# Two places for the softmax's scores, half banks on half chunks, a select in place of a mask product, and products of zeros on TensorE

## The chip, the cores and the metric

The kernel runs on one core of a Trainium2 chip. The core has a matrix engine (TensorE, PE in the profile), a vector engine (VectorE, DVE), an activation engine (ScalarE, ACT), a general engine (GpSimd, POOL), and a queue engine that issues most of the transfers (SyncE, SP). Each engine works through its own list of instructions in order. They meet through semaphores. TensorE reads from SBUF and writes its sums to PSUM, which has eight banks of 512 f32 columns on 128 partitions.

The metric is device time in microseconds. The times shown are medians of several runs. One further execution was profiled, and all views of the profile come from that one.

## The reference

The input is one sequence `x` of 2048 tokens with 128 features. Four blocks follow each other, each fed by a layernorm and added to `x`:

1. A state space mixer with 8 heads, 16 states and a convolution of 4 taps, with a gate.
2. Causal attention with 16 heads of 8 features, then a mixture of 8 experts. The block normalises its input once more, attends, adds, normalises again, and adds for each token the two experts that its router picks. All eight experts are computed and weighted, with zero for those not picked. An expert is 128 to 512 features, an exact GELU, and back to 128.
3. A Mamba scan with 256 channels and 16 states.
4. A gated network with ternary weights: two products 128 to 512 multiplied with each other, two layers 512 to 512 with GELU, and one back to 128.

What matters most here is the attention:

```
scores = where(causal, q @ k.T / sqrt(8), finfo.min)   # 16 heads, 2048 x 2048
out    = softmax(scores) @ v
```

and the fourth block:

```
h = silu(lin(x, w1)) * lin(x, w2)
h = gelu(lin(h, h1)); h = gelu(lin(h, h2)); return lin(h, w3)
```

## The kernel before, in words

The tokens are cut into four chunks of 512 (`C`). The kernel's functions are `ssd(c)` for block 1, `prepare`, `shift`, `weighted` and `conclude` for the attention, `experts(c)`, `scan(c, part)` on halves of 256 tokens, and `feed(c)` for block 4.

**The order is planned.** The functions do not issue instructions. They record operations in a `Program`, which notes which operation needs which. `Order.play` (line 534) then plays a simple timeline: each operation has a price from `_cost` (line 343), each engine takes the ready operation that can start first, and among equals the one with the longest chain behind it. Tiles get their place when their first operation is taken, so places of SBUF and PSUM are part of this play. The outcome is one fixed list per engine, which `Order.issue` (line 630) emits from line 638. That is why almost all instructions in the profile stand on line 638, and why they have to be told apart by their tiles. On the chip the lists do not change: where an instruction waits, everything behind it on its engine waits too.

**Attention.** For each chunk `c` and each group `g` of four heads there are two loops.

- `shift` (line 869) finds the row maxima. A pair of heads gives two products with 32 rows each into the tile `m` (two banks, one place). On diagonal blocks two bf16 products with `mask_qk` are added. VectorE reduces the 1024 columns to `top_a`.
- `weighted` (line 901) computes the scores again with keys on the partitions. A pair of heads takes the two products `ps_e<-qR,w_kR`, two more that add the shift (`ps_e<-sh,w_onesR`), and on diagonal blocks two bf16 products with `mask_kq`. ScalarE's exponential takes the tile `e` (two banks, **one** place) to `probs` (three places). After both pairs of a key block, four products `ps_o<-probs` add up the weighted values in the bank `o`, in `sum_up` (line 908).

An f32 product is recorded as two matmuls. In the profile `32*128` means that 32 rows of the array were used, `128*9` that 9 columns were.

**PSUM.** `m` and `e` have two banks each, `o` one. Three single banks `a`, `b` and `c` serve everything else, one tile per bank. The banks of `m`, `e` and `o` are lent to these when nobody waits for them (lines 665 to 700).

**SBUF.** The pool `second` (experts and scan) opens after `first` (block 1). The pool `last`, which holds all tiles of `feed`, opens after `attention` has been given up, so no `feed` can start before the attention has ended.

**Scan.** For each of 16 states VectorE multiplies and scans (`sdb`), GpSimd copies the last column (`hlast`), and a GpSimd transfer adds the result to one of two sums (`sL<-sdb`, 256 KB each). GpSimd's list also holds two short operations of each layernorm (`rs`).

The masked product and the exponential in `weighted`, which the change touches most:

```
for j in range(2 * diag):
    nc.tensor.matmul(pss[:, j, q0 : q0 + P], ident16, mask_kq, start=False, stop=True)
pr = tile_("probs", (P, 2, C))
nc.scalar.activation(pr[:, :, q0:], pss[:, :, q0:], AF.Exp, scale=...)
```

Of the kernel before, what the change touches and what calls it, by code (L numbers as in the profile page):

```python
# [76 lines left out]
class Place:  # L77


    def __init__(self, pool, banks=None, lent=None, real=None):  # L80
        self.pool, self.lent, self.real = pool, lent, real
        self.user, self.free = None, 0.0
        self.banks = banks or (self,)


class Tile_:


    def __init__(self, tag, shape, dtype, name, real=None):
# [3 lines left out]
        self.ops = set()  # L93
# [104 lines left out]
class Op:  # L198
    __slots__ = (
        "n", "engine", "calls", "deps", "time", "after", "table", "batch", "allots", "tiles",  # L200
        "rank", "waits", "outs", "start", "end", "ready",
# [3 lines left out]
class Program:  # L205
# [5 lines left out]
    def __init__(self, nc):  # L211
        self.nc, self.ops, self.tags, self.joined, self.batching = nc, [], {}, None, None
        for e in self.ENGINES:
            setattr(self, e, Engine(self, e))
# [14 lines left out]
    def add(self, engine, method, args, kw):  # L229
# [12 lines left out]
        for v, w in [(v, False) for v in reads] + [(v, True) for v in writes]:  # L242
# [21 lines left out]
            t.ops.add(op)  # L264
            op.tiles.add(t)
# [6 lines left out]
    def new(self, engine, table=None):  # L272
# [4 lines left out]
        op.n, op.deps, op.allots, op.tiles = len(self.ops), {}, [], set()  # L277
        self.ops.append(op)
        return op
# [104 lines left out]

class Order:
# [8 lines left out]
    def settle(self):  # L394
# [36 lines left out]
        for op in ops:  # L431
            for t in op.allots:
# [22 lines left out]
    def rank(self):  # L455
        ops = self.p.ops
        outs = {o: [] for o in ops}
        for o in ops:
# [3 lines left out]
            o.ready = 0.0  # L462
# [30 lines left out]
        for o in reversed(order):  # L493
# [5 lines left out]
            o.rank = r + o.after  # L499

    def possible(self, op):

        at, seen, taken = 0.0, {}, set()
        for t in op.allots:
# [7 lines left out]
            for pl in tag.places:  # L512
                if pl in taken or any(b.user is not None or b in taken for b in pl.banks):
                    continue
# [19 lines left out]
    def play(self):  # L534
        free = {e: 0.0 for e in Program.ENGINES}
        cand = {e: [] for e in Program.ENGINES}
# [13 lines left out]
        while len(self.order) < n:  # L550
            best = None
            for e, ops in cand.items():
# [3 lines left out]
                for o in ops:  # L556
                    at = max(free[e], o.ready)
# [10 lines left out]
                    if at < least:  # L568
                        least = at
                    pick.append((at, o))  # L570
                if not pick:
                    continue
                o = max((o for at, o in pick if at <= least + 1e-6), key=lambda o: self.key(o, open_batch))
# [8 lines left out]
            at, o = best  # L582
            e = o.engine
            cand[e].remove(o)
            for t in o.allots:
                t.tag.wanted -= 1
            if o.allots:
                self.possible(o)
                for t in o.allots:
                    t.tag.given += 1  # L590
                    for b in t.place.banks:
                        b.user = t
# [11 lines left out]
            o.start = at  # L604
            free[e] = at + time
            o.end = at + time - o.time + o.after
# [12 lines left out]
            for d, full in o.outs:  # L619
                d.waits -= 1  # L620
                d.ready = max(d.ready, o.end if full else o.start)
                if d.waits == 0:
                    enter(d)
            self.order.append(o)
        self.span = max(o.end for o in self.order)

# [14 lines left out]
SWITCH, BOOST = 1.28, 40.0  # L641
# [3 lines left out]
def two_layers(ctx: ExitStack, tc: tile.TileContext, a: dict, out: bass.AP):  # L645
# [19 lines left out]
    def banks(tag, bank, lent=None, width=1, shared=False):  # L665
        t = nc.tag(tag, width * C, True, shared)
        t.places.append(Place(None, bank.banks if isinstance(bank, Place) else tuple(bank), lent, None))
        return t.places[-1]

    pairs_ = {k: ps.tile([P, 2 * C], F32, name=f"ps_{k}") for k in ("m", "e")}  # L670
    single = {k: ps.tile([P, C], F32, name=f"ps_{k}") for k in ("o", "a", "b", "c")}
    bank = {}
    for k, t in pairs_.items():
        for j in range(2):
            bank[f"{k}{j}"] = Place(None, real=t[:, j * C : (j + 1) * C])
    for k, t in single.items():
        bank[k] = Place(None, real=t)

    def seat(tag, names, lent=None, width=1, shared=False, whole=None):
        t = nc.tag(tag, width * C, True, shared)  # L680
        pl = Place(None, tuple(bank[n] for n in names), nc.tags[lent] if lent else None)
        pl.real = whole if whole is not None else bank[names[0]].real
        t.places.append(pl)

    seat("m", ("m0", "m1"), width=2, whole=pairs_["m"])
    seat("e", ("e0", "e1"), width=2, whole=pairs_["e"])
    seat("o", ("o",))
    for n in ("a", "b"):
        seat("a", (n,), shared=True)
# [839 lines left out]
```

## Time and profile before

| | |
|---|---|
| median of 3 runs | 1730.93 us (1716.0 to 1738.16) |
| profiled execution | 1727.12 us, span 1725.4 us |
| mean granted TensorE clock | 0.785 |
| PE busy | 1503.1 us (87%), 6350 matmul records |
| DVE busy | 994.8 us (58%) |
| ACT busy | 642.9 us (37%), 56 table loads among it |
| POOL busy | 326.4 us (19%) |
| transfers | 91.75 MB, 53 GB/s mean |

The span is the time from the first to the last instruction; the profiled execution took 1.7 us more. "Busy" of PE counts the whole duration of each matmul record, including the time until its result has left the array, so 87% busy does not mean that the array streams for 87% of the time. The granted clock tells which share of its full rate TensorE was given.

Going by the tiles in the trace, block 1 alone fills the first 150 us. Attention runs from there to 1395 us, beside the rest of block 1 and beside experts and scans of chunks whose attention is done. The row maxima (`shift`) end at about 1210 us. From 1395 us on the kernel computes the last experts, the last two scan halves, and all four feeds.

### The profile page before, as it was taken

Reading aid. Unit: us, or ns where it says so; the run is one execution under the profiler, and the core shown is the slowest. Engines: PE = TensorE matmul, PEld = TensorE weight load, DVE = VectorE, ACT = ScalarE, POOL = GpSimd, SP = SyncE. Lnnn points to the kernel's source line nnn. Section 1 sums busy time; section 2 is a strip of 40 time slices with the busy share of each in tenths; the row PEclk is TensorE's granted clock in tenths of the full one; section 3 lists DMA queues with packets and bytes.
Section 4 is the critical chain, followed back from the end, with each engine's and each line's share of the span. In section 5 each row is a group of like instructions: output and inputs, shape, how many; then the busy total and the mean of one; then the engine's idle time right before and its main releaser. Section 6 shows DMA issues by size and latency. Waiting matters only on the chain. (4 is left out here: it accounts for less than half of the span.)

```text
span 1725.4 us, 17368 instructions
## 1 busy us (share of the span) xinstructions
PE 1503.1 (87%) x6350; PEld 670.9 (39%) x6350; DVE 994.8 (58%) x1874; ACT 642.9 (37%) x873; POOL 326.4 (19%) x458
## 2 busy tenths in 40 slices
PE   6899998999999998899998899899877679995738
PEld 3554554455423343333333243233322234442323
DVE  4556557665545468667867656775454551256641
ACT  2221421432334426445453433454445433234311
POOL 4321310310000111212311111121031221103320
PEclk9887987996879959987865655799565569997769
DMA  2000000000112102524402311341042543134730
GB/s 86 1 1 1 1 1 1 1 1 1 42 36 61 51 1 56 123 67 87 97 7 46 60 36 35 95 110 42 13 84 56 99 110 98 49 114 106 157 88 6
DMA packets 77334, 91.75 MB, mean 53 GB/s; under 512 B 7040, under 2 KB 47776, under 8 KB 77248
## 3 DMA queue, kind: packets, MB, share of 16 engines
q1 hardware_dynamic: 59536, 58.11, 11.4%
q0 software_dynamic: 17280, 31.46, 10.7%
q10 hardware_dynamic: 432, 1.06, 0.2%
q8 instruction: 50, 0.82, 0.2%
q14 instruction: 36, 0.29, 0.1%
HBM read 57.90 MB, written 1.25 MB: 34 GB/s over the span
## 5 line engine op out<-in xcount | busy, mean ns | idle before, releaser
L638 DVE TENSOR_REDUCE top_a_None<-ps_m 128x2 f32<-128x1024 f32 (+3 forms) x320 | 339.7, 1062 | 285.0 <-PE ps_m L638 278.4
L638 ACT ACTIVATE probs_attention<-ps_e 128x1024 f32<-128x1024 f32 (+3 forms) x320 | 286.5, 895 | 526.9 <-PE ps_o L638 281.2
L638 PE MATMUL ps_e<-qR_attention,w_kR_attention 32*128 32x512 f32 (+3 forms) x640 | 187.8, 581 | 82.5 <-ACT probs_attention L638 80.9
L638 PE MATMUL ps_m<-w_kR_attention,qR_attention 32*128 32x512 f32 (+3 forms) x640 | 178.3, 546 | 17.4 <-DVE top_a_None L638 16.1
L638 PE MATMUL ps_o<-probs_attention,w_vv_attention 128*9 128x512 f32 (+3 forms) x1152 | 182.6, 712 | 0.2 <-ACT probs_attention L638 0.2
L638 POOL DMA_DIRECT2D sL_second<-sdb_second x114 | 99.2, 885 | 385.6 <-DVE sdb_second L638 328.6
L638 PEld LDWEIGHTS ps_e<-qR_attention,w_kR_attention 32*128 32x128 f32 x640 | 74.0, 227 | 237.9 <-ACT probs_attention L638 187.5
L638 DVE TENSOR_TENSOR_SCAN sdb_second<-sda_second,w_hlast_None,sdb_second 128x256 f32<-128x256 f32 x212 | 149.6, 739 | 7.7 <-ACT sda_second L638 5.4
L638 PEld LDWEIGHTS ps_m<-w_kR_attention,qR_attention 32*128 32x128 f32 x640 | 71.6, 217 | 211.8 <-issue 67.9
L638 PE MATMUL ps_e<-sh_attention,w_onesR_attention 32*128 32x512 f32 (+3 forms) x640 | 148.6, 459 | 0.0
L638 PE MATMUL ps_c<-h_second,fc_second 128*128 128x512 f32 x208 | 114.9, 654 | 0.6 <-DVE ye_second L638 0.6
L638 ACT ACTIVATE sda_second<-sL_second 128x512 f32<-128x512 f32 x120 | 72.7, 624 | 31.8 <-DVE sdb_second L638 18.6
L638 ACT ACT_TABLE_LOAD x56 | 71.8, 1283 | 30.2 <-PE ps_a L638 18.6
L638 DVE TENSOR_TENSOR sdb_second<-sL_second,sbb_second 128x512 f32<-128x512 f32 x101 | 68.0, 680 | 24.0 <-DMA sL_second<-sdb_second 11.1
L638 PEld LDWEIGHTS ps_e<-sh_attention,w_onesR_attention 32*128 32x128 f32 x640 | 80.8, 249 | 0.5
L638 POOL TENSOR_TENSOR acc_second<-acc_second,ye_second 128x512 f32<-128x512 f32 x28 | 36.5, 1305 | 231.3 <-DVE ye_second L638 229.8
L638 PE MATMUL ps_a<-enT_second,fc_second 128*128 128x512 f32 x128 | 77.0, 686 | 3.1 <-ACT h_second L638 2.2
L638 ACT ACTIVATE h_second<-ps_a,cols 128x512 f32<-128x512 f32 x64 | 44.0, 687 | 63.3 <-PE ps_a L638 63.2
L638 POOL COPY w_hlast_None<-sdb_second 128x2 f32<-128x2 f32 x99 | 55.6, 570 | 23.8 <-DVE sdb_second L638 23.5
L638 PE MATMUL ps_b<-enT_second,fc_second 128*128 128x512 f32 x98 | 58.8, 686 | 0.9 <-ACT h_second L638 0.8
L638 PE MATMUL ps_m<-fh_last,hw_last 128*128 128x512 f32 x120 | 58.3, 608 | 0.2 <-DVE sW_second L638 0.2
L638 PEld LDWEIGHTS <-ident 128*128 128x128 bf16 x512 | 30.6, 101 | 61.7 <-issue 50.0
(430 smaller groups left out, 2094.3 us busy)
## 6 DMA issues: line engine op xcount, KB each, us to landing
sL_second<-sdb_second POOLq DMA_DIRECT2D x114, 256.0 KB, 3.6
fc_second<-in_fc SPq DMA_DIRECT2D x64, 256.0 KB, 2.6
sbb_second<-scratch_b SPq DMA_DIRECT2D x112, 128.0 KB, 3.0
gb_second<-scratch_g SPq DMA_DIRECT2D x32, 256.0 KB, 3.3
hw_last<-in_h SPq DMA_DIRECT2D x8, 1024.0 KB, 5.3
w_last<-in_w SPq DMA_DIRECT2D x12, 256.0 KB, 3.9
sbb_last<-scratch_b SPq DMA_DIRECT2D x16, 128.0 KB, 3.4
sL_second<-sdb_last POOLq DMA_DIRECT2D x6, 256.0 KB, 4.2
```

What stands on the lines that cost most here:

```text
L638: getattr(engine, method)(*args, **kw)
```

## The change

It has these parts.

- **Two places for `e`.** PSUM now has `m` (2 banks), `e` (4 banks, two places), `o` and `a`. The banks `b` and `c` are gone.
- **Half banks on half chunks.** A new tag `d` is half a bank (256 columns). `experts` and `feed` now work on 256 tokens at a time, `experts(c, part)` and `feed(c, part)`, and load their weights for each half. `feed` takes its weights in tiles of 256 KB (`fw`, three places in each pool) in place of 1 MB, and has places in `second` as well as in `last`.
- **Mask by a select.** The two `mask_kq` products are left out. After the exponential, GpSimd's `affine_select` sets the masked part of `probs` (128 by 2 by 128) to zero. `mask_qk` in `shift` stays.
- **Products of zeros.** The planner gets a model of the array (`Array`): how many of the array's cells each product uses, in windows of 3.41 us, and a clock that falls to half when the use is low. Where its PE would stand idle and the use of the last window is below `FILL` = 0.7, it puts in a bf16 product of the identity with 512 columns of zeros into a free bank. The built list has 467 of them: 375 go to the bank `a`, 75 to banks of `m`, 15 of `e`, 2 of `o`. 276 stand before the last attention product and 191 behind it.
- **Work moves from VectorE to ScalarE.** The last step of each layernorm, the copies and bias additions out of PSUM in `prepare`, `shift`, `weighted`, `conclude`, `scan` and `feed` become activations. Layernorm gets two more short GpSimd operations (`nm`). One scaling in `scan` goes from VectorE to GpSimd.
- `prepare` is split: the projections of the last two head groups (`project(c, 2)`) come when the chunk's attention starts. `qR` has two places in place of three.

All engines' lists are planned anew. Instructions in the built lists, before and after: ScalarE's table loads 56 and 81, the fetches of expert weights (256 KB each) 64 and 128, PE's bf16 products with a mask 512 and 256. The weights of `feed` were 8 fetches of 1 MB and 12 of 256 KB; they are 104 of 128 or 256 KB.

```diff
-    pairs_ = {k: ps.tile([P, 2 * C], F32, name=f"ps_{k}") for k in ("m", "e")}
-    single = {k: ps.tile([P, C], F32, name=f"ps_{k}") for k in ("o", "a", "b", "c")}
+    wide = {k: ps.tile([P, n * C], F32, name=f"ps_{k}") for k, n in (("m", 2), ("e", 4))}
+    single = {k: ps.tile([P, C], F32, name=f"ps_{k}") for k in ("o", "a")}
...
+    for j in (0, 2):
+        seat("e", (f"e{j}", f"e{j + 1}"), whole=wide["e"][:, j * C : (j + 2) * C])
     seat("o", ("o",))
...
+    for n, lent in (("a", None), ("m0", "m"), ("m1", "m"), ("e3", "e"), ("e2", "e"), ("e1", "e"), ("e0", "e"), ("o", "o")):
+        seat("a", (n,), lent)
+        for half in range(2):
+            seat("d", (n,), lent, half)
...
     def layernorm(z, dst, src, width=D):
...
+        nc.gpsimd.tensor_tensor(nm, mv[:, :, 0], rs, ALU.mult)
+        nc.gpsimd.tensor_scalar(nm, nm, -1.0, None, ALU.mult)
         for b in range(nb):
-            nc.vector.tensor_scalar(
-                dst[:, b, :], src[:, b, :], mv[:, b, 0:1], rs[:, b : b + 1], ALU.subtract, ALU.mult
+            nc.scalar.activation(
+                dst[:, b, :], src[:, b, :], AF.Identity, bias=nm[:, b : b + 1], scale=rs[:, b : b + 1]
             )
...
-                        nc.tensor.matmul(pss[:, j, q0:], onesR[hr], sh[hr, q0:], start=False, stop=not diag)
-                    for j in range(2 * diag):
-                        nc.tensor.matmul(pss[:, j, q0 : q0 + P], ident16, mask_kq, start=False, stop=True)
+                        nc.tensor.matmul(pss[:, j, q0:], onesR[hr], sh[hr, q0:], start=False, stop=True)
                 pr = tile_("probs", (P, 2, C))
...
+                if diag:
+                    select(pr[:, :, q0 : q0 + P], [[0, 2], [1, P]], 0, -1, ALU.is_ge, 0.0)
...
+class Array:
+    WINDOW = 3.41333
...
+            use, part = self.use.get(i - 1, 0.0) / self.WINDOW, self.part.get(i - 1, 0.0) / self.WINDOW
+            fast = FAST or use + 0.6 * part >= 0.33 if self.clocks[i - 1] == 1.0 else use >= 0.37
+            self.clocks[i] = 1.0 if fast else 0.5
...
+                if e == "tensor" and FILL and pe_left > 0 and self.zeroed(last_at):
+                    tf = max(pe.end + FGAP, last_at)
+                    if least > tf and pe.lately(tf) < FILL:
+                        for pl in self.p.tags["a"].places:
...
+                                spare = pl
+                                if best is None or tf < best[0]:
+                                    best = (tf, None)
...
     def filler(self, place):
...
+        op.calls = [("matmul", (t.view(), *self.zeros), {"start": True, "stop": True})]
...
-    def feed(c):
+    def feed(c, part):
...
+            if f % 2 == 0:
+                w12 = tile_("fw", (P, 2, 2 * P))
...
     for c in range(NC):
-        experts(c)
+        for part in range(SPLIT):
+            experts(c, part)
         for part in range(SPLIT):
             scan(c, part)
-        feed(c)
+            feed(c, part)
```

## The prediction

> **What bounds the kernel now.** I read the page first. TensorE (PE) is the busiest engine, 87%, and the row of its granted clock is full of fives and sixes.
>
> ```profile
> PE 1503.1 (87%) x6350; PEld 670.9 (39%) x6350; DVE 994.8 (58%) x1874; ACT 642.9 (37%) x873; POOL 326.4 (19%) x458
> ...
> PEclk9887987996879959987865655799565569997769
> ```
>
> Windows of 50 us read between 0.50 and 1.00, so I count all lowered time as half clock: the mean of 0.785 gives 2 x 0.215 x 1725 = 742 us of it. Next I cut the span into stretches by what runs in them. Columns: stretch, length, busy us of PE, its matmuls, clock, share of the DMA engines, GB/s.
>
> ```profile
> 0.00:150.00 150.00, 121.87 (x488) 0.87 0.08 25
> 150.00:650.00 500.00, 478.41 (x2494) 0.84 0.06 17
> 650.00:900.00 250.00, 226.69 (x960) 0.83 0.34 74
> 900.00:1100.00 200.00, 178.46 (x712) 0.55 0.23 47
> 1100.00:1210.00 110.00, 106.95 (x458) 0.93 0.33 81
> 1210.00:1395.00 185.00, 138.49 (x562) 0.55 0.30 60
> 1395.00:1550.00 155.00, 140.44 (x373) 0.94 0.34 96
> 1550.00:1725.40 175.40, 111.82 (x316) 0.79 0.42 93
> ```
>
> By 2 x (1 - clock) x length, half-clock time is 39, 160, 85, 180, 15, 167, 19 and 74 us. 900:1100 and 1210:1395 run at half clock almost throughout, though PE is busy for 89% and 75% of them. They hold thin attention products and hardly any dense expert products. The stretch between them, with dense products among the same attention, has 0.93. What the low clock costs is seen in the groups of these stretches, first 900:1100, then 1100:1210 (busy us, mean ns):
>
> ```profile
> L638 PE MATMUL ps_m<-w_kR_attention,qR_attention 32*128 32x512 f32 x96 | 36.0, 747 | 3.0 <-DVE top_a_None L638 3.0
> L638 PE MATMUL ps_o<-probs_attention,w_vv_attention 128*9 128x512 f32 x152 | 34.0, 982 | 0.0
> L638 PE MATMUL ps_e<-qR_attention,w_kR_attention 32*128 32x512 f32 x86 | 32.0, 742 | 14.4 <-ACT probs_attention L638 14.1
> ```
>
> ```profile
> L638 PE MATMUL ps_m<-w_kR_attention,qR_attention 32*128 32x512 f32 x62 | 16.2, 520 | 0.3 <-DVE top_a_None L638 0.3
> L638 PE MATMUL ps_o<-probs_attention,w_vv_attention 128*9 128x512 f32 x72 | 11.1, 694 | 0.0
> L638 PE MATMUL ps_e<-qR_attention,w_kR_attention 32*128 32x512 f32 x40 | 10.9, 540 | 1.3 <-ACT probs_attention L638 1.2
> ```
>
> Per pair of heads (two records of m or e, four of o) PE is busy 0.75, 0.89 and 0.74 us in the first, 0.52, 0.62 and 0.55 in the second: the same work in 0.71 of the time. Last the waits, in all and in the longest:
>
> ```profile
> POOL sL_second L638 <- DVE sdb_second L638: 328.6, 73, 19.3
> ACT probs_attention L638 <- PE ps_o L638: 281.2, 124, 5.4
> PE ps_e L638 <- ACT probs_attention L638: 81.4, 104, 2.8
> ```
>
> PE's own wait for the single place of e is 81.4 us, 42.4 of it in 1210:1395. So the bound is PE at a low clock until 1395 us. Behind that it is a chain: experts of the last chunk (1399 to 1491), two scan halves (to 1671), feed (to 1722).
>
> **A rule against the change.** PE's longest wait on the exponential is 2.8 us, and in 900:1100 the longest listed is 2.3 us, yet the clock there is 0.55. The Trainium skill, "TensorE: Matmul & The Clock Gate", section "HAM oscillation — how this bites in real kernels", gives the rule that no idle gaps over about 3.4 us keep the clock up. By it zeros in short gaps would bring nothing, and the sum below would come out about 140 us higher. The measured rows decide: here a busy but thinly used array is at half clock.
>
> **The change part by part,** against the profiled span of 1725.4 us (1727.1 with what lies around it; the median shown is 4 us more).
>
> *Clock.* Half-clock time, times PE's busy share there, times the 0.29 that full clock saves: 0:150 39 x 0.8 x 0.29 = 9; 150:650 160 x 0.96 x 0.29 = 45; 650:900 85 x 0.9 x 0.29 = 22; 900:1100 178 x 0.29 = 52, and 8 of its 21 us without PE busy; 1100:1210 4; 1210:1395 138 x 0.29 = 40 and 8 of waits that run at PE's pace. Sum 188. Zeros stand only where the plan expects idle, and only 276 lie ahead of the end of attention, so I take three quarters: **-141**. Ends: 0 (the use stays too low) and -188.
>
> *Zero products.* No row has 512 bf16 columns. Below, the bf16 mask with 128 columns: two in 0.28 us, 0.14 each. Above, an f32 record with 512 columns, which follows the next in 0.43 us at full clock (four records of ps_m in 1.88 us, two in 1.02). I take half the upper, 0.21, since an f32 record streams more than one pass: 467 x 0.21 = 98 us, ends 65 and 200. The cover is 222 us in which PE is not busy. That idle shrinks when the rest gets faster, and 101 of the zeros wait for the reader of their bank (an activation of 0.69 us, say) with PE's whole list behind them, so a quarter comes on the path: **+25**. If the cover is gone, +98.
>
> *Second place of e.* It removes PE's 81.4 us. In 1210:1395 nothing else fills the gap: -34 of 42. Elsewhere -25 of 39, since m and dense products partly follow anyway: **-59**. Late next is the place of probs: three as before, and ScalarE already waits 281 us for ps_o, which frees them. With the sums at 0.62 a pair beside an exponential of 1.02 us that wait is covered at full clock only. Ends: -10 and -81.
>
> *Mask.* 256 products, 41.1 us busy, leave PE: **-30**. 128 selects come to POOL. Selects of 128x128 took 0.29 to 0.48 us; twice the elements lie between 0.29 and 0.97, I take 0.6: 77 us on an engine that is 19% busy. But each stands between exponential and sum, behind whatever POOL waits for: **+10** (0 to the third rival's price).
>
> *Half chunks.* Expert and feed products have 256 columns: two records take the 0.43 us of one (w_u at 256 columns takes 502 and 405 ns for one record against 654 for 512, but those durations include the way out of the array), so no change in streaming. Past 1395 us, half the final feed (46 us, 1674 to 1720) goes ahead, -20; the first scan half needs half the experts (92 us), -25 of at most 46; the clock there, -10: **-55**. Ends: -100, and +100 by the second rival.
>
> *VectorE to ScalarE.* The rows that move add up to 128.6 us. DVE goes to about 890 us with the smaller pieces. ACT gets 129, about 44 for more pieces (128x256 takes 0.47 us, 128x512 0.69: 352 x 0.47 - 176 x 0.69), and 25 table loads of 1.283 = 32: about 850 us. Both fit beside any time above 1300 us. In 650:900 DVE is busy 185 of 250 us, so **-10**; the loads in the last stretch, **+5**. The 80 new short layernorm operations on POOL (0.23 to 0.49 us each, 18 to 39 us in all) are mostly under PE's work.
>
> *Transfers.* SP issues 470 in place of 282. The list puts fetches of `fw` between the scan's `sbb`; one waiting for its place holds those behind it. I cost this at nothing before 1395 us, where the DMA share stays at 0.34.
>
> Sum: -141 + 25 - 59 - 30 + 10 - 55 - 10 + 5 = -255, so 1727 - 255 = **1472**, rounded to 1470 us.
>
> **The rivals.**
>
> *Half clock stays.* The list is fixed. If the chip runs behind the plan, PE is not idle where the zeros stand, and a stretch that falls to half runs there until dense products come, as before from 1300 to 1400 us, where two windows of 50 us read 0.50. For: between the zeros lie runs of hundreds of attention products. Against: experts come in eight portions in place of four, so dense products are spread. With a third of the clock term (47 of 141) and half of the zeros on the path (49 in place of 25): 1472 + 94 + 24 = **1590**.
>
> *Transfers bound the last stretch.* Feed weights come twice, +11.5 MB, and the last experts +4.2 MB. After 1395 us 155 x 96 + 175 x 93 = 31 MB moved; 47 MB in 275 us is 170 GB/s, more than the densest fortieth of the span (157). The chain that ended last shows what a loaded queue does (start, length):
>
> ```profile
> 1633.42 4.98 DMA sL_second<-sdb_second
> ...
> 1644.60 5.19 DMA sL_second<-sdb_second
> ```
>
> The median landing of these sums is 3.6 us. The last two states' products on VectorE started at 1655.57 and 1661.41, 5.8 us apart, where their work is 0.69 + 1.39 = 2.1. If the 28 sums of the last two halves go so, they add 28 x 3.7 = 104 us in place of the 55 gained: 1472 + 55 + 104 = **1630**.
>
> *Slower: selects behind POOL's waits.* POOL waits 328.6 us in 73 waits for the scan's VectorE work, 4.5 us each. In the new list many selects stand right behind such a transfer. While one waits, ps_o waits, and with it all that follows on PE. If each of the 128 selects costs 2.0 us more than in my sum, the gain of 255 is gone; from 2.3 us on the change is slower by over 2%. At 2.9 us: 1472 + 371 = **1840**. Against: a quarter of the selects belong to the first chunk, where no scan runs yet.
>
> *It does not do what it says:* two places, but ScalarE waits for probs instead. Then 49 of the 59 stay: 1520, inside my case.
>
> *Better:* full clock throughout and PE closer packed, 1330: the busy time at full clock, 1503 - 742 x 0.29 - 41 + 98 = 1345, is near that floor.
>
> **How the numbers follow.** Forecast 1470 (1390 to 1540): 0.45. Half clock stays, 1540 to 1650: 0.22. Transfers, 1540 to 1680: 0.10. Better, under 1390: 0.10. Slower: 0.09. Unmoved, by parts that cancel: 0.04. The range from 1350 to 1680 leaves out some 0.06 below and 0.13 above. Within 2%, 1696 to 1766, is about what a measurement here can tell from no change: 0.04. Faster 0.87, slower 0.09.
>
> **What would show it.** Right: a clock of 0.88 or more; no stretch of 100 us at 0.55; PE's wait on probs for e under 30 us; zero products near 0.21 us apart; attention ending near 1200 us. Wrong: fives in the clock row between the first and the last expert products; POOL selects idle for long behind DVE sdb with ps_o waiting on POOL; DMA share above 0.7 at the end with states 5 us apart.

## The result, and the profile after

The changed kernel took 1815.1 us (median of 4 runs, 1790.43 to 1830.07), the kernel before 1724.18 us beside it. The ratio is 1.047, with an interval of 1.033 to 1.061: slower, where I had forecast 1470 us. A ratio, here and below, is taken over the executions within 1.5% of the fastest of their kernel, so it is not quite the quotient of the medians.

The profiled execution took 1813.19 us, its span is 1811.5 us and its mean granted clock 0.857 (before: 0.785). First the page, with the same two rows as before, and the group of the zero products (busy us, mean ns, then the idle time of PE just before them):

```profile
PE 1521.4 (84%) x7343; PEld 821.4 (45%) x7393; DVE 908.8 (50%) x1726; ACT 811.4 (45%) x1342; POOL 446.3 (25%) x731
...
PEclk9699977989869999965798766798998889998887
...
L811 PE MATMUL ps_a<-zeros,ident 128*128 128x512 bf16 x338 | 114.7, 451 | 58.8 <-ACT h_second L811 32.2
```

The clock row has lost most of its fives, and VectorE (DVE) and ScalarE (ACT) have nearly the busy times I had worked out (890 and 850). Yet the sum is longer. The windows, cut where the stages changed (stretch, length, the busy us of PE, of its weight loads, of DVE, ACT and POOL, then clock, share of the DMA engines, GB/s):

```profile
900.00:1100.00 200.00, 172.27 (x852) 80.86 (x859) 120.80 (x197) 106.37 (x161) 45.14 (x79) 0.82 0.30 70
...
1375.00:1600.00 225.00, 170.63 (x664) 119.79 (x670) 91.20 (x191) 86.93 (x174) 62.01 (x95) 0.90 0.51 123
1600.00:1811.50 211.50, 161.62 (x615) 106.19 (x621) 56.11 (x109) 51.27 (x102) 25.32 (x32) 0.84 0.40 99
```

The stretch 900:1100 has 0.82 where it had 0.55. But the last product of the attention ends at 1362 us (before: 1388), not near 1200, and what is left then takes 449 us in place of 338. In those 449 us no engine is busy for more than 76% of the time, and the clock is at 0.87: that stretch waits. Both stretches, from the first weighted sum to the last and from there to the end, in the same columns:

```profile
181.00:1362.00 1181.00, 1030.55 (x5437) 508.44 (x5460) 681.26 (x1196) 616.30 (x961) 292.16 (x491) 0.85 0.24 56
1362.00:1811.50 449.50, 340.05 (x1321) 230.23 (x1331) 155.45 (x325) 144.34 (x288) 94.99 (x143) 0.87 0.47 113
```

The waits, in all, how many, the longest (us). The last answers the 81.4 us of before, the one above it the 281.2 us; the first two are new in this size:

```profile
ACT h_second L811 <- PE ps_a L811: 177.6, 106, 5.3
...
PE ps_a L811 <- ACT h_second L811: 78.9, 102, 1.4
...
ACT probs_attention L811 <- PE ps_o L811: 69.6, 40, 6.2
...
PE ps_e L811 <- ACT probs_attention L811: 38.2, 58, 1.8
```

PE waits 102 times for ScalarE to have read `h`'s bank, and ScalarE 106 times for PE. Two engines that wait for each other at this rate take turns. The timeline shows how, first in an expert's first layer (start, length, engine, instruction, idle time before it and what ended that):

```profile
1262.79 0.84 ACT L811 ACTIVATE h_second<-ps_a,cols 128x256 f32<-128x256 f32 x2 [1.22 <-PE ps_a L811]
...
1263.68 1.13 PE L811 MATMUL ps_a<-enT_second,fc_second 128*128 128x256 f32 x4 [0.87 <-ACT h_second L811]
1264.85 0.84 ACT L811 ACTIVATE h_second<-ps_a,cols 128x256 f32<-128x256 f32 x2 [0.75 <-PE ps_a L811]
...
1265.74 1.13 PE L811 MATMUL ps_a<-enT_second,fc_second 128*128 128x256 f32 x4 [0.93 <-ACT h_second L811]
1266.91 0.84 ACT L811 ACTIVATE h_second<-ps_a,cols 128x256 f32<-128x256 f32 x2 [1.22 <-PE ps_a L811]
```

PE writes both halves of bank `a`, ScalarE reads both, PE writes both again; nothing lies side by side, though with two places PE could fill one while the other is read. In a feed three engines go round in this way, 1.72 us for each turn (from one start of PE to the next, 1687.81 to 1689.53):

```profile
1687.29 0.47 ACT L811 ACTIVATE fs_second<-ps_a,w_half_s_None 128x256 f32<-128x256 f32 x1 [1.79 <-DVE fxn_second L811]
...
1687.81 0.70 PE L811 MATMUL ps_a<-fnT_second,fw_last 128*128 128x256 f32 x2 [1.12 <-ACT fs_second L811]
1688.55 0.42 DVE L811 SCALAR_TENSOR_TENSOR fs_second<-fs_second,ps_a 128x256 f32<-128x256 f32 x1 [1.30 <-PE ps_a L811]
1689.01 0.47 ACT L811 ACTIVATE fs_second<-ps_a,w_half_s_None 128x256 f32<-128x256 f32 x1 [1.25 <-DVE fs_second L811]
1689.53 0.70 PE L811 MATMUL ps_a<-fnT_second,fw_last 128*128 128x256 f32 x2 [1.02 <-ACT fs_second L811]
```

PE's product at 1687.81 writes the half that nobody reads any more (it becomes the `p1` of the next 128 features), and waits for the activation on the other half (the `p1` of these features). VectorE's step at 1688.55 needs only this `p1` and the activation, both done at 1687.76, and waits for PE.

**What the built program says.** A wait on another engine in it names one instruction of that engine. I looked, for each such wait of an instruction that touches PSUM, at what would have to be waited for if only the same addresses counted, then if the whole bank counted, then if the whole PSUM tile counted. Kernel before: 22 waits exist only because a bank is shared (all between ACT and DVE), 33 only because a tile of several banks is. After: **333** for a shared bank, and **190** for a shared tile. An example of the second sort: a score product into columns 0 to 511 of `ps_e`, the first place, waits for the exponential that reads columns 1024 to 2047, the second place. `ps_e` is one tile of four banks.

So both of the new sorts of place have a snag that I had not seen: halves of a bank exclude each other, and so do the two places of the scores. PE's wait on the exponentials fell all the same, from 81.4 to 38.2 us, but nothing came to lie side by side. For the second sort the trace has a plain count: in the changed kernel not one of the 320 exponentials has a score product running beside it, the same as before, when there was one place.

The Trainium skill, "PSUM — Partial Sum Buffer", section "PSUM bank collisions raise a hardware error", asks for waits by bank (and quadrant of partitions), not by address. The 333 waits are of this kind. The 190 between banks of one tile go beyond it. No run here shows what a collision would do.

### The profile page after: what moved, and what is told of

It is laid out like the page before. It is cut to its first block, busy times and chain, and to the rows that moved or that the text cites. A ratio compares the mean times of both kernels' runs of the same rounds, so it can differ in the third digit from the quotient of the medians.

```text
span 1811.5 us, 20345 instructions
## 1 busy us (share of the span) xinstructions
PE 1521.4 (84%) x7343; PEld 821.4 (45%) x7393; DVE 908.8 (50%) x1726; ACT 811.4 (45%) x1342; POOL 446.3 (25%) x731
## 5 line engine op out<-in xcount | busy, mean ns | idle before, releaser
L811 ACT ACTIVATE h_second<-ps_a,cols 128x256 f32<-128x256 f32 x232 | 100.1, 471 | 186.1 <-PE ps_a L811 177.6
L811 PE MATMUL ps_a<-enT_second,fc_second 128*128 128x256 f32 x428 | 142.3, 451 | 34.0 <-ACT h_second L811 29.3
L811 PE MATMUL ps_a<-zeros,ident 128*128 128x512 bf16 x338 | 114.7, 451 | 58.8 <-ACT h_second L811 32.2
L811 PE MATMUL ps_e<-qR_attention,w_kR_attention 32*128 32x512 f32 (+3 forms) x640 | 121.5, 494 | 36.2 <-ACT probs_attention L811 35.4
L811 POOL TENSOR_SCALAR_AFFINE_SELECT probs_attention<-probs_attention 128x256 f32<-128x256 f32 x128 | 60.0, 474 | 312.2 <-ACT probs_attention L811 311.2
L811 POOL TENSOR_TENSOR acc_second<-acc_second,ye_second 128x256 f32<-128x256 f32 x56 | 46.2, 824 | 346.5 <-DVE ye_second L811 330.6
L811 PE MATMUL ps_a<-h_second,fc_second 128*128 128x256 f32 x360 | 115.6, 447 | 13.9 <-ACT h_second L811 7.2
L811 PEld LDWEIGHTS ps_a<-enT_second,fc_second 128*128 128x128 f32 x428 | 80.3, 211 | 82.5 <-ACT h_second L811 50.7
L811 PE MATMUL ps_e<-sh_attention,w_onesR_attention 32*128 32x512 f32 (+3 forms) x640 | 99.8, 399 | 0.0
L811 PEld LDWEIGHTS ps_a<-h_second,fc_second 128*128 128x128 f32 x360 | 72.4, 219 | 41.7 <-ACT h_second L811 12.4
```

What stands on the lines that cost most here:

```text
L811: getattr(engine, method)(*args, **kw)
```

## The experiments

Times are medians. Every kernel was timed beside the kernel before, whose median lay between 1713.7 and 1731.9 us. A difference of two times in the text can carry some of that: by the ratios the 96 us below are 79, the 93 are 99, and the 80 that half chunks cost are 72. The 0.971 of the run with whole chunks is the quotient of the medians; its four executions took 1645.6 to 1691.38 us, so differences from it hold to some 25 us. "Bank" and "tile" count the two sorts of wait in the built program.

| run | us | ratio to before, interval | bank | tile |
|---|---|---|---|---|
| changed kernel | 1815.1 | 1.047 (1.033 to 1.061) | 333 | 190 |
| no zeros, planned anew | 1812.0 | 1.050 (1.037 to 1.062) | 348 | 186 |
| whole chunks | 1681.3 | 0.971, no interval | 81 | 202 |
| banks apart | 1728.3 | 1.006 (1.001 to 1.011) | 127 | 360 |
| one place for the scores | 2104.0 | 1.217 (1.206 to 1.229) | 307 | 264 |
| scores in two tiles | 1719.1 | 1.002 (0.997 to 1.006) | 332 | 59 |
| two tiles, whole | 1609.7 | 0.936 (0.927 to 0.944) | 81 | 66 |
| two tiles, whole, apart | 1529.4 | 0.891 (0.885 to 0.897) | 44 | 142 |
| two tiles, whole, no zeros | 1553.6 | 0.905 (0.897 to 0.913) | 80 | 66 |
| two tiles, apart, half chunks | 1609.5 | 0.933 (0.926 to 0.941) | 125 | 177 |
| all three, no zeros | 1524.5 | 0.886 (0.880 to 0.892) | 49 | 127 |
| all three, mask by products | 1629.3 | 0.947 (0.939 to 0.955) | 47 | 120 |
| all three, one place | 1573.7 | 0.915 (0.907 to 0.922) | 5 | 79 |
| two tiles, same order, apart | 1626.3 | 0.944 (0.939 to 0.949) | 153 | 191 |
| all three, experts halved | 1577.6 | 0.916 (0.910 to 0.922) | 130 | 148 |
| all three, no select, no mask | 1625.3 | 0.944 (0.939 to 0.950) | 43 | 133 |
| all three, VectorE again | 1593.2 | 0.925 (0.919 to 0.930) | 45 | 139 |
| changed, zeros dropped | 1818.3 | 1.046 (1.034 to 1.057) | 345 | 186 |
| all three, zeros dropped | 1540.2 | 0.893 (0.886 to 0.900) | 46 | 139 |

"Two tiles", "whole", "apart" are the edits shown below (scores in two tiles, whole chunks, a free bank first); "all three" has all of them.

**The planner makes a caveat.** Where an edit changes the operations or the rules for places, all lists are planned anew, and the order by itself can move the time by tens of us. Five runs are free of it: each keeps the order of another kernel to the instruction (scores in two tiles, twice; tiles moved in the same order; zeros dropped, twice).

### One part of the change undone

The first four runs undid one part each (the code shows excerpts: `...` marks lines left out in between, and an edit can have further lines around an excerpt). Theory A was that the halves of a bank exclude each other; B that the zeros cost; C the transfers; D the banks taken by the second place.

No zeros:

```diff
-SWITCH, BOOST, BURST, FAST, PAIR, ZMIN, ZWAIT, FILL, FGAP = 1.28, 40.0, 0.0, False, 0.0, 0.0, 0.0, 0.7, 0.03
+SWITCH, BOOST, BURST, FAST, PAIR, ZMIN, ZWAIT, FILL, FGAP = 1.28, 40.0, 0.0, False, 0.0, 0.0, 0.0, 0.0, 0.03
```

> The changed kernel with no product of zeros at all (467 planned ones left out; the rest of the plan is made anew, nothing else is edited). Theory A, two halves of one bank make PE and its readers take turns: the zeros are a side matter; without them PE gets back the 112 us that they streamed, the clock falls from 0.857 towards 0.80 and the real streaming takes some 60 us more again (1142 to about 1200), so the time stays within 40 us of 1815. Rival B, the zeros themselves are what cost: the zeros' 112 us and the 59 us of idle time before them go and the clock matters less: 1700 to 1740.

1811.96 us at a clock of 0.815: within the 40 us of theory A, and not as B.

Whole chunks for experts and feeds:

```diff
-        for part in range(SPLIT):
-            experts(c, part)
+        experts(c)
         for part in range(SPLIT):
             scan(c, part)
-            feed(c, part)
+        feed(c)
```

> The changed kernel with the experts and the feeds on whole chunks again, with the buffers and the weight loads that they had before; the second place of the scores, the select, the zeros and the half banks for the small tiles stay. Theory A (half banks shared): the large tiles fill whole banks, so PE and the readers do not take turns any more; the last stretch falls from 436 us towards the 330 us of before, the whole to 1690 to 1730. Rival C (the weights, fetched twice as often in small pieces, hold the last stretch): the same 1690 to 1730, so this run alone does not tell A from C. Rival B (zeros cost): 1790 to 1830.

1681.27 us, 134 less than the change, a little better than expected. From the end of the attention on 377 us in place of 449.

A free bank first:

```diff
+                now = max(since, *(b.free for b in pl.banks))
+                if tag.psum and tag.shared:
+                    for b in pl.banks:
+                        now = max(now, b.mate.free)
+                    cost = (any(b.mate.user is not None and b.mate not in pl.banks for b in pl.banks), now)
...
+                if best is None or cost < best[0]:
+                    best = (cost, now, pl)
```

> The changed kernel, where a tile that takes one bank or half of one is put into the bank whose other half is unused and that has been free longest, not into the first free place of the list; chunks stay halved, weights are fetched as in the change, zeros stay. In the plan the tiles that stand beside a live tile in the same bank fall from 557 to 303. Theory A: the last stretch falls from 436 us to 340 to 380 us, the whole to 1710 to 1760, and PE's waits on ACT's reads of h, fs and fh fall to half. Rival C (transfers): the last stretch stays at 420 or more, the whole at 1790 to 1830. Rival B (zeros): the same 1790 to 1830.

1728.33 us, 87 less, and the last stretch is 377 us: theory A, with all fetches as in the change, so C is out as its main cause. PE's waits for ScalarE to read `h`, `fs` and `fh` fall from 99.5 to 49.5 us, to half, as theory A had it. (The plan that ran has 280 such tiles, not 303.)

One place for the scores, the other two banks (still in the tile of four) for single tiles:

```diff
-    for j in (0, 2):
-        seat("e", (f"e{j}", f"e{j + 1}"), whole=wide["e"][:, j * C : (j + 2) * C])
+    seat("e", ("e0", "e1"), whole=wide["e"][:, 0 : 2 * C])
...
-    for n, lent in (("a", None), ("m0", "m"), ("m1", "m"), ("e3", "e"), ("e2", "e"), ("e1", "e"), ("e0", "e"), ("o", "o")):
+    for n, lent in (("a", None), ("e2", None), ("e3", None), ("m0", "m"), ("m1", "m"), ("e1", "e"), ("e0", "e"), ("o", "o")):
```

> The changed kernel with one place of two banks for the softmax's scores, as before, and the other two banks given to the single tiles from the start, as before. Theory A (and my forecast's step of 59 us for the second place): attention ends 40 to 80 us later, while the last stretch stays as it is; 1840 to 1890. Rival D (the banks that the second place takes from the other tiles are what the kernel lacks): faster than the change, 1740 to 1790.

2103.95 us: far outside of both. The loss lies in the attention, 1450 us from the first weighted sum to the last in place of 1181; the last stretch is 452 us. 289 us is no price of a second place. What the count of waits offers is that single tiles now lie in the same tile as the scores and exclude them: 264 waits of that sort in place of 190. That is an argument, not a test of this kernel; but it led to the next run.

### The scores in two tiles

```diff
-    wide = {k: ps.tile([P, n * C], F32, name=f"ps_{k}") for k, n in (("m", 2), ("e", 4))}
+    wide = {k: ps.tile([P, n * C], F32, name=f"ps_{k}") for k, n in (("m", 2), ("e", 2), ("f", 2))}
```

> The changed kernel, instruction for instruction in the same order, but the two places of the scores are two tiles of two banks and no longer the two halves of one tile of four banks. Counted in the built program, 190 waits among the engines that touch PSUM name an instruction on another bank of the same tile; here 59 are left. Theory E (the second place is partly undone by such waits: PE's products into one place wait for ScalarE's exp that reads the other): the stretch of the attention, 1181 us, becomes 30 to 80 us shorter, the whole 1735 to 1785. Rival F (ScalarE and PE are in turn there anyway, so that the wait that is left ends at nearly the same moment): within 15 us of 1815.

**1719.05 us, 96 less** (79 by the ratios), with the same instructions in the same order, and better than both theories had it. Of 320 exponentials 98 now have score products beside them. The timeline of this run shows one: the exponential reads the place `f` while PE fills the place `e`. The second view is the changed kernel's: there the exponential reads the second place of `ps_e`, and the product, into the first, starts when the exponential ends.

```profile
609.93 1.02 ACT L811 ACTIVATE probs_attention<-ps_f 128x1024 f32<-128x1024 f32 x1
...
610.33 0.40 PE L811 MATMUL ps_e<-qR_attention,w_kR_attention 32*128 32x512 f32 x2
...
610.56 0.40 PE L811 MATMUL ps_e<-sh_attention,w_onesR_attention 32*128 32x512 f32 x2
```

```profile
640.12 1.04 ACT L811 ACTIVATE probs_attention<-ps_e 128x1024 f32<-128x1024 f32 x1
...
641.22 0.50 PE L811 MATMUL ps_e<-qR_attention,w_kR_attention 32*128 32x512 f32 x2 [1.45 <-ACT probs_attention L811]
```

Its waits on both places of the scores, which add up to 6.0 us for PE (38.2 before the split):

```profile
PE ps_e L811 <- ACT probs_attention L811: 3.5, 8, 0.6
...
PE ps_f L811 <- ACT probs_attention L811: 2.5, 2, 1.6
```

The gain is where theory E had it. From the first weighted sum to the last the attention takes 1101 us in place of 1181; the last stretch is as long as it was, 450 us. Here are both stretches of this run, to be compared with the next kernel's:

```profile
176.00:1277.00 1101.00, 978.45 (x5438) 495.69 (x5462) 679.46 (x1197) 616.12 (x962) 293.98 (x491) 0.89 0.25 60
1277.00:1726.60 449.60, 337.56 (x1317) 228.96 (x1329) 154.85 (x325) 144.59 (x288) 94.52 (x142) 0.88 0.46 113
```

### The same order, tiles moved to other banks

After the plan is made, a pass goes through its order and moves single tiles (the zeros' too) to a free bank where nothing lies beside them. No instruction changes its place in a list.

```diff
+        for t in sorted(tiles, key=lambda t: where[t][0][0]):
...
+                beside = [u for b in pl.banks if b.mate not in pl.banks for x, y, u in used.get(b.mate, ()) if x <= hi and lo <= y]
...
+                cost = (len(beside), last)
+                if best is None or cost < best[0]:
+                    best = (cost, pl)
```

> The run at 1719 us (the changed kernel's own order, the scores in two tiles) with that order kept for every instruction, zeros too; only afterwards 550 of the small tiles are moved to another free bank, so that waits that only a shared bank asks for fall from 332 to 153 in the built program (those for another bank of the same tile rise from 59 to 191). Theory A (halves of one bank take turns, and that costs): 1630 to 1690, the gain mostly in the last stretch (450 us). Rival G (what helped in the runs with other places was the other plan, not the places): 1705 to 1735.

**1626.29 us, 93 less again** (99 by the ratios; theory A, 4 us below its range), and this time the last stretch gives it: 359 us in place of 450, the attention stays at 1105.

```profile
165.00:1270.00 1105.00, 987.90 (x5466) 499.33 (x5460) 679.74 (x1196) 615.66 (x961) 292.54 (x491) 0.88 0.25 59
1270.00:1628.60 358.60, 299.16 (x1335) 218.23 (x1335) 155.63 (x325) 144.05 (x288) 96.16 (x143) 0.95 0.57 142
```

DVE and ACT are busy as long as they were, and the same fetches now come at 142 GB/s, in less time: the transfers had not been what held the stretch. Nor was it the zeros in the shared banks: the idle time of PE just before them is 65 us in the run before and 60 us here. In an expert's first layer PE now writes one tile while ScalarE reads another:

```profile
1300.03 1.03 PE L872 MATMUL ps_m<-enT_second,fc_second 128*128 128x256 f32 x4
1300.23 0.47 ACT L872 ACTIVATE h_second<-ps_a,cols 128x256 f32<-128x256 f32 x1
...
1300.89 0.59 PE L872 MATMUL ps_f<-enT_second,fc_second 128*128 128x256 f32 x2
1301.09 0.84 ACT L872 ACTIVATE h_second<-ps_m,cols 128x256 f32<-128x256 f32 x2 [0.39 <-PE ps_m L872]
```

The two runs together take back 189 us of the changed kernel (178 by the ratios) without moving an instruction. The count of waits for a shared tile went up in the second run, so the count alone is no price: what seems to matter is whether a wait closes a circle like the two above.

### What the half chunks cost by themselves

These four put the edits shown so far together; the last has whole chunks for the feeds alone:

```diff
         for part in range(SPLIT):
             experts(c, part)
         for part in range(SPLIT):
             scan(c, part)
-            feed(c, part)
+        feed(c)
```

> Whole chunks for experts and feeds, as in the run at 1681 us, and the two places of the scores as two tiles; the order of the instructions is that of the run at 1681 us. Theory E: 1600 to 1650, with the gain in the stretch of the attention (1121 us there). Rival F: 1665 to 1695.

1609.71 us: the two tiles gain 72 us with whole chunks too (50 between the fastest executions of the two), in the range of theory E, and 67 us of it lie in the attention (1054 us in place of 1121).

> The one before, and the small tiles put into the bank that is unused and longest free. Waits that only a shared bank asks for fall from 81 to 44 in the built program, but those for another bank of the same tile rise from 66 to 142. Theory A (halves of a bank take turns): 10 to 40 us faster than the run before it in this call; rival (both sorts of wait cost alike, and whole chunks leave few of the first): within 15 us of it or slower.

1529.35 us, better than both expected; planned anew, so part of the 80 us may be order.

> Scores in two tiles, small tiles in the bank that is free, but experts and feeds on half chunks as in the change: against the run at 1529 us it puts back the half chunks alone, with few waits for shared banks left. If the half chunks themselves help, as my forecast's step of 55 us said, once the banks don't hold them: 1470 to 1510. If they cost by their own (twice the weight loads and fetches, more instructions): 1570 to 1630. If the shared banks were all that was wrong with them: within 20 us of 1529.

1609.53 us: with two tiles and free banks first, half chunks are 80 us slower than whole ones, in the middle of "cost by their own". They are not quite alone in this: the program has 125 waits for a shared bank in place of 44, and its order is another. No stretch of this run is read here.

> Scores in two tiles, small tiles apart, experts on half chunks, feeds on whole chunks: between the run with both on whole chunks (1529 us) and the one with both on half chunks (1610 us). If the feeds' halves cost the 80 us (their weights are fetched anew for each half): 1520 to 1550. If the experts' halves do (64 more weight loads of 256 KB and shared banks): 1580 to 1620.

1577.63 us, below the 1580 to 1620 expected for the experts: their halves cost 48 of the 80 us, which leaves 32 for the feeds' halves. The half experts bring the waits for a shared bank from 44 back to 130, so this need not all be twice the loads.

### The zeros

Planned anew without them, the kernels differ by order as well:

> Whole chunks, two tiles for the scores, and no products of zeros. If the zeros do what my forecast said (a clock gain of some 100 us against 25 us of their own): 60 to 110 us slower than the second run of this call. If what they take of PE's time equals what the clock gives back, as in the run of the change without zeros (1812 against 1815): within 30 us of it, at a granted clock lower by 0.04 to 0.07. If they only cost: 60 us or more faster.

> Two tiles for the scores, whole chunks, small tiles apart, no zeros. By the pair at 1610 and 1554 us (zeros cost 56 us there): 1460 to 1500. If the zeros cost only where false waits stand about them: within 20 us of 1529. If the clock needs them: 1560 to 1620.

1553.62 us (56 less than with them, between two of the outcomes expected) and 1524.48 us (5 less, inside the noise). So two kernels kept their order, and only left the zeros out when the order was issued:

```diff
+        self.order = [o for o in self.order if o.n >= 0]
```

> The changed kernel's own order, with the 467 products of zeros left out after the order was made and nothing else moved. My forecast's step: the clock's gain is lost and 25 us of the zeros come back, so 1815 plus 60 to 110. If what they give and take is equal, as in the run planned anew without them (1812): 1790 to 1835. If they only cost (112 us of streaming, partly on the path): 1720 to 1770.

> The same for the version at 1529 us (scores in two tiles, whole chunks, small tiles apart): its own order without its 424 products of zeros. Equal give and take, as in the one planned anew (1524): 1510 to 1550. Zeros needed: 1570 to 1630. Zeros only cost: 1440 to 1490.

1818.32 us against 1815.1, and 1540.22 against 1529.35: equal give and take in both. The clock did fall, from 0.857 to 0.821 and from 0.915 to 0.869. The next table tells what it did to the time. It is an estimate from the trace: each record of a product counts with the distance at which such records follow each other at full clock (0.43 us for a full f32 record of 512 columns, 0.22 for 256 columns or a zero product; thin products, which run side by side, their part of it), divided by the clock granted at its moment. "Rest" is the time of the span that is left.

| us of the profiled span | products | zeros | rest |
|---|---|---|---|
| before | 1228 | 0 | 498 |
| changed kernel | 1142 | 112 | 557 |
| changed, zeros dropped | 1188 | 0 | 602 |
| scores in two tiles | 1093 | 106 | 528 |
| two tiles, same order, apart | 1082 | 112 | 435 |
| two tiles, whole, apart | 1042 | 89 | 401 |
| the same, zeros dropped | 1087 | 0 | 451 |

The zeros speed up the products by 46 us and take 112 us, of which only 45 were free. The last row but one against the last says the same (45, 89 and 50). Two limits: by the first pair the kernel without zeros should be 21 us faster, as its profiled execution was (a span of 1790.3 us against 1811.5), but the medians say 3 us slower, so the estimate is good to some 20 us. And the trace of the changed kernel holds 417 of the 467 zeros; those missing count as rest, so 112 and 45 may both be some 13 us too low, which leaves their difference as it is.

### Mask, second place, VectorE

Two runs with all three edits and without the select; the first adds the mask by products again, the second has no mask:

```diff
+                    for j in range(2 * diag):
+                        nc.tensor.matmul(pss[:, j, q0 : q0 + P], ident16, mask_kq, start=False, stop=True)
...
-                if diag:
-                    select(pr[:, :, q0 : q0 + P], [[0, 2], [1, P]], 0, -1, ALU.is_ge, 0.0)
```

> Like the run at 1529 us, but the mask of the scores is added by products again and not made by a select of POOL on the exponentials. My forecast's steps: 30 us of products back, 10 us of selects gone: 1540 to 1560. If the selects lie on the path (POOL behind ScalarE, PE behind POOL): 1480 to 1515.

> Like the run at 1529 us with neither the select nor the products that add the mask: the mask of the scores is left out, so the output is another. Undoing the select for the products took 100 us (1629). If the products cost that (PE's own 30 us and a switch of shape for each): 1500 to 1530 here. If it is the order that the plan comes to without a select behind each exponential: 1590 to 1640 here too.

1629.28 and 1625.29 us: 100 us slower with the mask's products than with the select, but 96 us slower also with neither. These two differ by 4 us, so the products are hardly what costs the 100 us, which lie in the attention (1094 and 1080 us in place of 998). What is left as a cause is the order that the plan comes to; that is an argument, and I can't say what in the order. The first result is outside of both ranges expected. What the select itself is worth stays open.

One place for the scores, and two banks as single tiles of their own:

```diff
-    for j, k in ((0, "e"), (2, "f")):
-        seat("e", (f"e{j}", f"e{j + 1}"), whole=wide[k])
+    seat("e", ("e0", "e1"), whole=wide["e"])
```

> Like the run at 1529 us, but with one place for the scores, the other two banks as single tiles of their own. My forecast's step for the second place, 59 us with ends of 10 and 81: 1540 to 1610, most likely 1590. If the second place is worth what undoing it in the change took (289 us): 1750 or more. If single banks are worth more: below 1529.

1573.69 us: where the two places are truly two, the second is worth 44 us, less whatever the other order makes of it. The loss lies in the attention (1055 us in place of 998); the last stretch is 17 us shorter.

VectorE for what had moved to ScalarE (one of thirteen places; the scaling in `scan` comes back from GpSimd too, and the two short GpSimd operations of each layernorm go):

```diff
-                nc.scalar.activation(dst[:, j], pf[:, j], AF.Identity, bias=col(f"b{n}", g + j))
+                nc.vector.tensor_scalar(dst[:, j], pf[:, j], col(f"b{n}", g + j), None, ALU.add)
```

> Like the run at 1529 us, with the layer norms' last step, the copies and the additions of biases on VectorE again instead of ScalarE. My forecast's step: 10 us slower, 1535 to 1550. If VectorE is what the scans wait for, 1560 to 1600. If ScalarE was the worse place: below 1515.

1593.19 us: 64 us slower, six times my step, in the range expected if the scans wait for VectorE. That it is the scans is not shown: the attention takes 1080 us in place of 998, but the last stretch is shorter (343 us in place of 365). This run, too, is planned anew.

## Why the prediction was wrong

**Second place of e** ("It removes PE's 81.4 us ... -59"). Failed. I took a second place in the plan for a second place in the built program. There 190 waits tie banks of one tile together, no exponential ever had a score product beside it, and undoing this with the order kept gave 96 us (79 by the ratios). Where it works, the place came out at 44 us in plans made anew, inside my bounds of 10 to 81.

**Half chunks** ("no change in streaming ... -55"). Failed, and the largest. The streaming was right: 256-column records follow at 0.216 us. But streaming was not the question. A half bank is no place of its own: 333 waits exist because halves share a bank, and moving tiles apart, with the order kept, gave 93 us (99). What I had counted as a gain at the end (half the last feed ahead, half the experts before the first scan half) does not show either: with the scores in two tiles and 125 waits for a shared bank left, half chunks are 80 us slower than whole ones. I had looked up what a bank of half the size costs the writer, and not who else must keep off the bank.

**Clock and zeros** (-141 and +25). The direction was right: the clock rose to 0.857, and the stretch at 0.55 is gone. But of the 742 us of half clock 516 are left, so a third is gone where I had taken three quarters of all that lay before 1395 us. The streaming of the products became shorter by 86 us, not 141. Of these the zeros make 46, and of the other 40 some 16 are the mask's products that are gone (982 us of products at full clock before, 966 after). The zeros cost 67 us beyond free time (112 - 45), not 25, and 58.8 us of idle time lie before those in the bank `a`, most of it for the reader of a bank. As a pair they are worth nothing in either kernel, where my sum had 116 us. What I cited against the term, the rule of the Trainium skill, "TensorE: Matmul & The Clock Gate", section "HAM oscillation — how this bites in real kernels", speaks of gaps over some 3.4 us. PE idles for longer than that 8 times without the zeros (63.5 us in all) and 3 times with them (26.5 us), while its half-clock time is 640 and 516 us, so such gaps are the smaller part of it; the clock fell by 0.036 and 0.046 without the zeros. The rule's outcome for the time, no gain, was the right one all the same.

**Mask** (-30 and +10). Not confirmed: the two runs without the select differ by 4 us with and without the products, and the select's worth is hidden by the plan's order.

**VectorE to ScalarE** (-10). Right direction, 64 us in the fast version, planned anew, instead of 10.

**The rivals.** "Half clock stays" had the size of the clock term (47 us; the zeros make 46) and the wrong time, 1590 us, since it kept the other terms. "Slower: selects behind POOL's waits" did not happen: the loads of PE wait 7.1 us in all for POOL's `probs`. "Transfers bound the last stretch" named the right stretch, but the same fetches passed in 359 us once the banks were free. "It does not do what it says" named the right part and gave the wrong reason (ScalarE waiting for `probs`) and a price of 10 us. No rival had PSUM itself as the thing waited for.

That the version with two tiles, whole chunks and free banks, 1529 us, is close to my sum without its half-chunk term (1472 + 55) is no confirmation: the terms in it came out quite differently.

Open are the worth of the select, the share of the order in every comparison that was planned anew, and why one place in the tile of four banks cost 289 us.

## What to carry to other kernels

Count a new place in PSUM only after looking at the built program's waits: which instruction does the next writer wait for, and does it touch the same columns? Here halves of one bank and banks of one wide tile gave places that the planner used and the waits of the built program took back, and giving each place of the scores its own tile, at no cost in instructions, made 96 us. Fill work that raises a clock has to be weighed against the idle time that is truly there, by dropping it with the order kept.

## What the runs showed of the hardware

The same 966 us of products (at full clock, by the estimate above) streamed in 1142 us in the changed kernel and in 1093 us when only the scores' tile was split: with fewer waits the clock is higher as well (0.890 in place of 0.857), so a removed wait was worth more than its length: PE's waits on the exponentials fell by 32 us (38.2 to 6.0), the span by 85 us. And 142 GB/s over 359 us in the last stretch, at a DMA share of 0.57, came with the shortest such stretch of the kernels read here that have both experts and feeds on half chunks.
